# Layer 2's result and layer 3's exponentials turned by way of DRAM, with two small groups and orders of their own for the first and last period

## The chip, the core and the metric

The kernel runs on one core of one Trainium2 chip. A core has five engines with an instruction stream each: the tensor engine (PE), the vector engine (DVE), the scalar engine (ACT), GpSimd (POOL) and the sync engine (SP), which here only issues transfers. Each stream runs in the order in which it was written; between streams there are semaphores. The time is that of the device, in microseconds. Before the change it was 3014.07 (the median of three runs, 3013.18 to 3015.02).

## The reference

Four graph layers run one after the other on 128 independent graphs. A graph has 128 nodes with 256 features (`x`, 128 x 128 x 256, f32) and an adjacency matrix of zeros and ones (`adj`). After every layer stands a residual and a layer norm, `x = norm(x + layer(x))`.

- Layer 0 is graph attention with four heads of 64 features: scores from two vectors per head, leaky relu, a mask by `adj`, softmax, a weighted sum, elu.
- Layer 1 is a gated graph network of three steps. Each step multiplies the state by a weight matrix, sums over neighbours and runs a GRU cell with 256 units. This is most of the arithmetic.
- Layer 2 sums neighbours by relation and multiplies by one matrix per relation, plus a bias. With adjacency values of 0 and 1 only one relation occurs. A general loop behind the main one is run only if a larger value is met.
- Layer 3 is graph attention with one head.

## The kernel before

**Groups and stages.** The 128 graphs go in 32 groups of four (`G`, L25). A group passes four stages, each a Python generator that yields after every small step: `loads` (L124), `head` (layer 0, L348), `body` (layer 1, L437) and `tail` (layers 2 and 3, L573). Before the first period stand, in straight code, the loading of all weights on SP (L137 to L173), the constants on DVE (score columns of `w0` and `w3`, selection matrices, halved biases, L175 to L202) and `fold_weights` (L208), which multiplies layer 1's three matrices into the GRU's input weights: `wc`.

**The order.** The order of work is written out by hand. `STEPS` (L41) is a string of letters, one per step; `LETTERS` (L46) gives each letter a stage and the group relative to the period. `advance` (L688) runs one step. The same string serves all 36 periods, those at the ends too; steps of groups that don't exist fall out. `fold_weights` stands in one piece before period 0. At the end of the main code (L704) every instruction is tied to the one before it on its engine, so that the written order is each engine's order.

**Turning.** PE contracts over the partition dimension, so the kernel needs many 128 x 128 blocks both ways round. It has two ways. PE transposes against an identity matrix (`transpose`, L85), into PSUM, from where ACT or DVE copies or adds. Or the block goes through DRAM: SP writes it out (`to_dram`, L224), four transfers read it back so that 32 x 32 squares lie rearranged (`from_dram`, L234, `squares`, L98), and one DVE instruction transposes all 32 x 32 squares. `turn_rows` (L240) uses the second way for `x1` and `x3`, and the first for the first group's `x1` and the last group's `x3` (`by_pe`). Layer 0's exponentials also go through DRAM, except in the first group (L388, L392, L406).

**The lines that the change touches most.** At the start of `tail` PE turns the last hidden state `h3T` (`hT`), and DVE adds it to `x1` out of PSUM (L577 to L583). Towards its end PE turns layer 3's exponentials `em` and ACT copies them (L664 to L670). In `body`, whose code the change leaves nearly alone, a step's gates are matmuls of 512 columns (four graphs of 128 nodes), L476 to L481; each is two instructions in the trace. `softmax_unscaled` (L312) holds slope, maximum and exponentials. `layernorm` (L261) holds the statistics on DVE, a power on POOL and the scaling on ACT.

**Buffers.** PSUM has four banks for gates and four for all else. `sq`, where squares arrive, is a ring of four; the DRAM buffers `turn` are a ring of four; `x1` and `x3` have two each, `adj` five. The weights that only the folding needs lie in buffers that tail and body use later (`hr`, `xb`, `x3T_0`, `wh3`, `x2_0`).

Of the kernel before, what the change touches and what calls it, by code (L numbers as in the profile page):

```python
# [16 lines left out]
P = 128  # L17
# [22 lines left out]
AHEAD, BEHIND = 2, 2  # L40
STEPS = """  # L41
ucnbbmbggggcbbuucugcglggcccccbbbblbbbbgbbtbuubbbggbbbbggutbttbbubbbbtuttuububutubbbbbbbbgbttggttubbu
uubguhttttbubgtguubbbbbuubtttbbbtbttbttthggggghhhhhhgbhhbbhtgbbbbbbbbgbbbbbbbggghthghtbgggbbbgbtbbtt
ttttbtttbbbbbbbbbbbbbbhghbgthhub
"""
LETTERS = {"b": ("b", 0), "c": ("b", -1), "h": ("h", 2), "g": ("h", 1), "l": ("l", 2), "m": ("l", 1), "n": ("l", -1), "t": ("t", -1), "u": ("t", -2)}  # L46
ORDER = [LETTERS[s] for s in STEPS if s in LETTERS]

@with_exitstack
def kernel(ctx: ExitStack, tc: tile.TileContext, a: dict, out: bass.AP):
# [3 lines left out]
    NG = B // G  # L56
# [50 lines left out]
    def load_adj(st):  # L107
        st["adj"] = ring(sp, [P, G, N], I32, "adj", f"adj_{st['g']}", 5)
        nc.sync.dma_start(st["adj"], adj[st["graphs"]].rearrange("g n m -> n g m"))

    def load_rows(st):
        st["x0"] = sp.tile([P, G, D], F32, tag="x0", name=f"x0_{st['g']}")
        nc.sync.dma_start(st["x0"], x[st["graphs"]].rearrange("g n d -> n g d"))

    def load_x_squares(st):
        st["x0s"] = sp.tile([P, C, G * N], F32, tag="x0s", name=f"x0s_{st['g']}")
        for c in range(C):
            squares(st["x0s"][:, c, :], x[st["graphs"]].rearrange("g n d -> (g n) d")[:, ts(c, P)])

    def load_adj_squares(st):  # L120
        st["adj_s"] = sp.tile([P, G * N], I32, tag="adj_s", name=f"adj_s_{st['g']}")
        squares(st["adj_s"], adj[st["graphs"]].rearrange("g n m -> (g n) m"))
# [7 lines left out]
    def state(g):  # L130
        return {"g": g, "graphs": slice(g * G, (g + 1) * G), "relations": 1, "first": g == 0, "last": g == NG - 1}
# [3 lines left out]


    w0 = cp.tile([P, C, D + 2 * H], F32, tag="w0", name="w0")  # L137
    nc.sync.dma_start(w0[:, :, :D], a["L0_gnn_W"].rearrange("(c p) o -> p c o", p=P))
    vec = ring(sp, [P, 4, D], F32, "y", "vec", 2)
    nc.sync.dma_start(vec[:, 0, :], a["L0_gnn_a_src"].rearrange("h f -> (h f)").partition_broadcast(P))  # L140
    nc.sync.dma_start(vec[:, 1, :], a["L0_gnn_a_dst"].rearrange("h f -> (h f)").partition_broadcast(P))
    load_x_squares(states[0])
    load_adj(states[0])

    w1 = []
    for l, tag in enumerate(("hr", "xb", "x3T_0")):
        w1.append(sp.tile([P, C, D], F32, tag=tag, name=f"w1_{l}"))
        nc.sync.dma_start(w1[l], a["L1_gnn_weight"][l].rearrange("(c p) o -> p c o", p=P))
    wih = []
    for e, tag in enumerate(("wh3", "x2_0")):  # L150
        wih.append(sp.tile([P, 3 * D], F32, tag=tag, name=f"wih_{e}"))
        nc.sync.dma_start(wih[e], a["L1_gnn_w_ih"][e * P : (e + 1) * P, :])
    load_rows(states[0])
    whh = cp.tile([P, C, 3 * D], F32, tag="whh", name="whh")
    nc.sync.dma_start(whh, a["L1_gnn_w_hh"].rearrange("(c p) o -> p c o", p=P))
    bih = cp.tile([P, 3 * C], F32, tag="bih", name="bih")
    nc.sync.dma_start(bih, a["L1_gnn_b_ih"])
    bhh = cp.tile([P, 3 * C], F32, tag="bhh", name="bhh")
    nc.sync.dma_start(bhh, a["L1_gnn_b_hh"])
    w3 = cp.tile([P, C, D + 2], F32, tag="w3", name="w3")  # L160
    nc.sync.dma_start(w3[:, :, :D], a["L3_gnn_W"].rearrange("(c p) o -> p c o", p=P))
    nc.sync.dma_start(vec[:, 2, :], a["L3_gnn_a"][0, :D].partition_broadcast(P))
    nc.sync.dma_start(vec[:, 3, :], a["L3_gnn_a"][0, D:].partition_broadcast(P))
# [3 lines left out]
    def load_w2(t, r):  # L167
        nc.sync.dma_start(t, a["L2_gnn_weight"][r].rearrange("(c p) o -> p c o", p=P))
        return t

    load_w2(w2, 0)
    b2 = cp.tile([P, D], F32, tag="b2", name="b2")
    nc.sync.dma_start(b2, a["L2_gnn_bias"].partition_broadcast(P))  # L173

    for i in range(4):  # L175
        for c in range(C):
            w, nh = (w0, H) if i < 2 else (w3, 1)
            prod = ring(sp, [P, D], F32, "n", f"prod_{c}_{i}", 2)
            nc.vector.tensor_mul(prod, w[:, c, :D], vec[:, i, :])
            lo = D + i % 2 * nh  # L180
            nc.vector.tensor_reduce(w[:, c, lo : lo + nh], prod.rearrange("p (h f) -> p h f", h=nh), AX.X, ALU.add)

    identb = cp.tile([P, P], BF16, tag="identb", name="identb")
    nc.vector.tensor_copy(identb, ident)
    picks = {}
    for S in (G * H, G):
        one = ring(sp, [3 * S, S], F32, "pick", f"one_{S}", 2)  # L190
        nc.vector.tensor_add(one, ident[: 3 * S, :S], ident[: 3 * S, S : 2 * S])
        nc.vector.tensor_add(one, one, ident[: 3 * S, 2 * S : 3 * S])
        picks[S] = cp.tile([3 * S, S, P], BF16, tag=f"pick{S}", name=f"pick_{S}")
        nc.vector.tensor_copy(picks[S], one.unsqueeze(2).to_broadcast([3 * S, S, P]))


    bhalf = cp.tile([P, 2 * C], F32, tag="bhalf", name="bhalf")
    nc.vector.tensor_add(bhalf, bih[:, : 2 * C], bhh[:, : 2 * C])
    nc.vector.tensor_scalar(bhalf, bhalf, 0.5, None, ALU.mult)

    bhn = cp.tile([P, C], F32, tag="bhn", name="bhn")
    nc.vector.tensor_scalar(bhn, bhh[:, 2 * C :], 0.5, None, ALU.mult)  # L202

    wc = cp.tile([P, L, C, 3 * D], F32, tag="wc", name="wc")

    def fold_weights():  # L208
        for l in range(L):
            w1T = ring(sp, [P, C, D], F32, "agT", f"w1T_{l}", 4)  # L210
            for e in range(C):
                ps = bank(C, P)
                for c in range(C):
                    transpose(ps[:, c, :], w1[l][:, c, ts(e, P)])
                nc.scalar.copy(w1T[:, e, :].rearrange("p (c d) -> p c d", c=C), ps)
            for c in range(C):
                for lo, hi in ((0, 512), (512, 3 * D)):
                    ps = bank(hi - lo)
                    for e in range(C):
                        matmul(ps, w1T[:, e, ts(c, P)], wih[e][:, lo:hi], start=e == 0, stop=e == C - 1)  # L220
                    nc.vector.tensor_copy(wc[:, l, c, lo:hi], ps)


    def to_dram(name, *parts):  # L224

        d = ring(dp, [sum(part.shape[1] for part in parts) * P, P], F32, "turn", f"d_{name}", 4)
# [13 lines left out]
    def turn_rows(st, x, tag, name, bufs, by_pe):  # L240

        if by_pe:
            yield
            yield
            t = ring(sp, [P, C, G * N], F32, tag, name, bufs)
            for c in range(C):
                ps = bank(G, N)
                for g in range(G):
                    transpose(ps[:, g, :], x[:, g, ts(c, P)])
                nc.scalar.copy(t[:, c, :].rearrange("p (g n) -> p g n", g=G), ps)  # L250
        else:
# [4 lines left out]
            t = ring(sp, [P, C, G * N], F32, tag, name, bufs)  # L256
# [4 lines left out]
    def layernorm(y, st, name, bufs=1):  # L261

        g0 = st["g"]
        sums = ring(sp, [P, G, 6], F32, "st", f"st_{name}_{g0}", 4)
        mv = ring(sp, [P, G, 2], F32, "mv", f"mv_{name}_{g0}", 4)
        rs = ring(sp, [P, G], F32, "rs", f"rs_{name}_{g0}", 4)
        mr = ring(sp, [P, G], F32, "mr", f"mr_{name}_{g0}", 4)

        def half(k):
            for g in range(k, k + 2):  # L270
                nc.vector.bn_stats(sums[:, g, :], y[:, g, :])  # L271

        def rest():
            for g in range(G):
                nc.vector.bn_aggr(mv[:, g, :], sums[:, g, :])
            nc.vector.tensor_scalar(rs, mv[:, :, 1], EPS, None, ALU.add)
            nc.gpsimd.tensor_tensor(rs, rs, neghalf[:, :G], ALU.pow)  # L277
# [3 lines left out]
            o = st[name] = ring(sp, [P, G, D], F32, name, f"{name}_{g0}", bufs)  # L281
            for g in range(G):
                nc.scalar.activation(  # L283
                    o[:, g, :], y[:, g, :], AF.Identity, bias=mr[:, g : g + 1], scale=rs[:, g : g + 1]
                )
# [5 lines left out]
    def residual_elu_norm(y, xin, st, name, layer, bufs=1):  # L291
# [3 lines left out]
        halves = [slice(k, k + 2) for k in range(0, G, 2)]  # L295
        ts_ = []
        for s in halves:
            t = ring(sp, [P, 2, D], F32, "elu", f"elu_{layer}_{g0}_{s.start}", 2)
            ts_.append(t)
            nc.vector.tensor_scalar(t, y[:, s], 0.0, None, ALU.min)  # L300
            yield
            nc.scalar.activation(t, t, AF.Exp)
            yield
        for s, t in zip(halves, ts_):
            nc.vector.scalar_tensor_tensor(t, y[:, s], 0.0, t, ALU.max, ALU.add)  # L305
            nc.vector.scalar_tensor_tensor(y[:, s], t, -1.0, xin[:, s], ALU.add, ALU.add)  # L306
            yield
            half(s.start)
# [3 lines left out]
    def softmax_unscaled(em, nm, den, cols):  # L312
# [4 lines left out]
        for r, i in enumerate(range(cols.start, cols.stop)):  # L317
# [3 lines left out]
            if r % 4 == 3:  # L321
                yield

    def as_rows(st, cols, name):

        h = cols.shape[2]
        t = ring(sp, [P, 3, G, h], BF16, "split", f"split_{name}", 2)
        r = ring(sp, [P, G, h], F32, "rest", f"rest_{name}", 2)
# [7 lines left out]
        nc.tensor.transpose(ps, t.rearrange("p k g h -> p (k g h)"), identb)  # L336
# [5 lines left out]
    def absent(adj_t, name):  # L342
        nbias = ring(sp, [P, G, N], F32, "nbias", f"nbias_{name}", 2)
# [4 lines left out]
    def head(st):  # L348

        g0, adj_t = st["g"], st["adj"]  # L350
        by_pe = st["first"]
        xT = sp.tile([P, C, G * N], F32, tag="x0T", name=f"x0T_{g0}")
# [4 lines left out]
        if st["relations"] < R:  # L357
            above = sp.tile([P, G, N], F32, tag="adj_T", name=f"above_{g0}")
            nc.scalar.activation(above, adj_t, AF.Relu, bias=negone, accum_out=unmet[:, g0 : g0 + 1])
        yield  # L360
        wh = sp.tile([P, G, D + 2 * H], F32, tag="wh0", name=f"wh0_{g0}")
        for g in range(G):
            ps = bank(D + 2 * H)
            for c in range(C):
# [408 lines left out]
```

## Time and profile before

| | us |
|---|---|
| median of three runs | 3014.07 |
| profiled execution | 3011.99 |
| its span, from the first to the last instruction | 3010.1 |
| PE busy | 2935.0 |
| DVE busy | 1974.9 |
| ACT busy | 1335.4 |
| POOL busy | 494.2 |
| transfers on queue 1 | 34.7% of 16 engines |

A row of the profile names the line of the code, the engine, the operation, the tile written and the tiles read, the shapes and how often it occurs; then the busy time, the mean of one in nanoseconds, the idle time of the engine just ahead of it and what ended that. PEld is PE's loading of the stationary operand, beside the matmuls. "L83" and "L86" are the helpers `matmul` and `transpose`, so the tiles tell such rows apart: `ps<-ident,h3T` is the turning of the last hidden state, `gate<-agT,wc` a gate's part from the neighbours. `SPq` is a transfer issued from SP. In a timeline, several equal instructions in a row are one line: start, time from the first start to the last end, engine, line, operation and count. Ends of matmuls are modelled; starts are measured.

### The profile page before, as it was taken

How to read it: one execution, taken by the hardware profiler on the slowest of the kernel's cores; microseconds unless marked ns; L12 is line 12 of the kernel's file. 1: busy time of each engine (PE TensorE's matmuls, PEld its weight loads, DVE VectorE, ACT ScalarE, POOL GpSimd, SP SyncE). 2: the span in 40 equal slices, each digit the busy share in tenths (PEclk: the TensorE clock that was granted, in tenths of full speed). 3: DMA queues.
4: the chain of work that ended last, by engine and by line, in shares of the span. 5: the costliest groups of instructions: out<-in, count | busy, mean ns of one | idle time of the engine just before them, and what ended most of it. 6: DMA issues, size and time to landing. Idle time of an engine off the chain costs nothing.

```text
span 3010.1 us, 33610 instructions
## 1 busy us (share of the span) xinstructions
PE 2935.0 (98%) x11166; PEld 1707.9 (57%) x11166; DVE 1974.9 (66%) x4393; ACT 1335.4 (44%) x3307; POOL 494.2 (16%) x456
## 2 busy tenths in 40 slices
PE   4999999999999999999999999999999999999995
PEld 3555556555556555556555556555556555556553
DVE  4556676766676766676766676766676766666654
ACT  2344444444444444444444444444444444444433
POOL 0011111111111111111111111111111111111111
PEclk7999999999999999999999999999999999999997
DMA  3243433334433333423343423333433343433310
GB/s 86 39 74 67 84 64 67 60 74 74 84 63 67 60 75 73 84 63 67 60 76 72 85 63 67 60 76 71 84 64 67 60 76 72 84 63 67 63 29 15
DMA packets 902614, 203.24 MB, mean 68 GB/s; under 512 B 723617, under 2 KB 901921, under 8 KB 902433
## 3 DMA queue, kind: packets, MB, share of 16 engines
q1 hardware_dynamic: 902432, 201.01, 34.7%
q8 instruction: 90, 1.47, 0.2%
q14 instruction: 92, 0.75, 0.1%
HBM read 119.15 MB, written 81.79 MB: 67 GB/s over the span
## 4 chain that ended last, share of the span: by engine, by line
PE 97%; DVE 1%; ACT 0%; SPq 0%; issue 0%; DMA 0%; POOL 0%; DVEq 0%; ACTq 0%; POOLq 0%
PE gate L83 66%; PE ps L83 27%; PE ps L86 4%; PE psb L336 0%; DMA vec<-in_L_gnn_a_dram 0%; ACT em L318 0%; SPq L102 0%; DVE em L382 0%; DVE st_x L271 0%; DVE elu L305 0%; DVE y L306 0%; DVE em L314 0%; DVE nm L315 0%; POOL rs_x L277 0%; DVE y L677 0%
## 5 line engine op out<-in xcount | busy, mean ns | idle before, releaser
L83 PE MATMUL gate<-agT,wc 128*128 128x512 f32 x2304 | 1098.8, 592 | 0.8 <-DVE agT L434 0.8
L83 PEld LDWEIGHTS gate<-agT,wc 128*128 128x128 f32 x2304 | 427.6, 190 | 438.6 <-issue 415.7
L83 PE MATMUL gate<-h2T,whh 128*128 128x512 f32 x768 | 372.6, 601 | 0.0
L83 PE MATMUL gate<-h1T,whh 128*128 128x512 f32 x768 | 366.3, 592 | 0.0
L83 PE MATMUL gate<-h0T,whh 128*128 128x512 f32 x768 | 361.0, 592 | 0.0
L318 ACT ACTIVATE em<-em,nm 128x128 f32<-128x128 f32 x640 | 247.0, 388 | 211.4 <-DVE nm L315 211.4
L494 DVE SCALAR_TENSOR_TENSOR n<-r,n 128x512 f32<-128x512 f32 x192 | 132.2, 689 | 209.1 <-ACT n L492 209.1
L508 DVE SCALAR_TENSOR_TENSOR d<-z,d 128x512 f32<-128x512 f32 x192 | 132.3, 689 | 186.8 <-ACT z L486 114.4
L283 ACT ACTIVATE x<-y,mr_x,rs_x 128x256 f32<-128x256 f32 x384 | 199.0, 590 | 84.2 <-DVE mr_x L279 83.9
L500 ACT ACTIVATE n<-n,bih 128x512 f32<-128x512 f32 x192 | 138.1, 719 | 209.7 <-DVE n L498 209.0
L502 POOL TENSOR_TENSOR d<-h2T,n 128x512 f32<-128x512 f32 x64 | 81.3, 1270 | 897.5 <-ACT n L500 897.5
L83 PEld LDWEIGHTS gate<-h0T,whh 128*128 128x128 f32 x768 | 140.9, 190 | 152.6 <-issue 152.3
L434 DVE COPY agT<-ps 128x512 f32<-128x512 f32 x192 | 129.9, 676 | 146.5 <-PE ps L83 146.4
L83 PEld LDWEIGHTS gate<-h2T,whh 128*128 128x128 f32 x768 | 138.3, 190 | 144.1 <-issue 138.7
L83 PEld LDWEIGHTS gate<-h1T,whh 128*128 128x128 f32 x768 | 138.5, 190 | 137.7 <-issue 130.3
L486 ACT ACTIVATE z<-gate,bhalf 128x512 f32<-128x512 f32 x192 | 130.7, 681 | 188.0 <-PE gate L83 188.0
L83 PEld LDWEIGHTS ps<-wh,aT 128*128 128x128 f32 x1280 | 174.5, 196 | 41.7 <-issue 22.0
L492 ACT ACTIVATE n<-gate,bhn 128x512 f32<-128x512 f32 x192 | 131.5, 685 | 139.0 <-PE gate L83 139.0
L83 PE MATMUL ps<-wh,aT 128*128 128x64 f32 (+1 forms) x1280 | 187.3, 299 | 5.8 <-DVE aT L404 4.9
L486 ACT ACTIVATE r<-gate,bhalf 128x512 f32<-128x512 f32 x192 | 131.6, 685 | 101.3 <-PE gate L83 101.3
L502 POOL TENSOR_TENSOR d<-h0T,n 128x512 f32<-128x512 f32 x64 | 86.6, 1352 | 529.6 <-ACT n L500 529.6
L498 DVE TENSOR_TENSOR n<-n,gate 128x512 f32<-128x512 f32 x192 | 131.6, 685 | 50.9 <-PE gate L83 47.4
(112 smaller groups left out, 4025.8 us busy)
## 6 DMA issues: line engine op xcount, KB each, us to landing
d_em<-em SPq DMA_DIRECT2D x62, 512.0 KB, 3.4
sq_em<-d_em SPq DMA_DIRECT2D x248, 128.0 KB, 4.3
x0s<-in_x_dram SPq DMA_DIRECT2D x256, 64.0 KB, 2.6
x<-in_x_dram SPq DMA_DIRECT2D x32, 512.0 KB, 4.1
out_dram<-o SPq DMA_DIRECT2D x32, 512.0 KB, 4.4
d_h0T<-x SPq DMA_DIRECT2D x62, 256.0 KB, 2.8
sq_h0T<-d_h0T SPq DMA_DIRECT2D x124, 128.0 KB, 3.5
d_x3T<-x SPq DMA_DIRECT2D x62, 256.0 KB, 2.7
```

The source lines that it names most:

```text
L83: nc.tensor.matmul(ps, lhsT, rhs, start=start, stop=stop)
L86: nc.tensor.transpose(ps, src, ident)
L283: nc.scalar.activation(o[:, g, :], y[:, g, :], AF.Identity, bias=mr[:, g : g + 1], scale=rs[:, g : g + 1])
L318: nc.scalar.activation(em[:, r, :], em[:, r, :], AF.Exp, bias=nm[:, i : i + 1], accum_out=den[:, i : i + 1])
L434: nc.vector.tensor_copy(into[c], ps.rearrange("p g n -> p (g n)"))
L486: nc.scalar.activation(t, gate[name][0], AF.Tanh, bias=bhalf[:, col : col + 1], scale=0.5)
L492: nc.scalar.activation(n, gate["nh"][0], AF.Identity, bias=bhn[:, c : c + 1], scale=0.5)
L494: nc.vector.scalar_tensor_tensor(n, tr, 1.0, n, ALU.add, ALU.mult)
L498: nc.vector.tensor_add(n, n, gate["ni"][0])
L500: nc.scalar.activation(n, n, AF.Tanh, bias=bih[:, 2 * C + c : 2 * C + c + 1])
L502: nc.gpsimd.tensor_sub(d, hT[:, c, :], n)
L508: nc.vector.scalar_tensor_tensor(d, tz, 1.0, d, ALU.add, ALU.mult)
```

## The change

1. **Sizes.** The groups are now one of two graphs, 31 of four, one of two: 33. All tiles and loops take the group's own size `n`; where a step has nothing to do in a small group, it yields all the same.
2. **h3 by way of DRAM.** In all groups but the last, SP writes the two halves of `h3T` to DRAM and reads them back as squares, DVE transposes them, and POOL adds `x1` in two instructions. The last group still turns on PE.
3. **em3 by way of DRAM.** The same for layer 3's exponentials: one write, four reads, one DVE instruction, which takes the place of four PE transposes and ACT's copy. The last group still uses PE.
4. **Orders.** The first period (`START`) and the last (`END`) have strings of their own, and the middle (`STEPS`) a new one in which more stages overlap: tails of the groups 1, 2 and 3 back, heads of this group and the two ahead.
5. **Constants and folding as stages.** They are generators too, letters in `START`, so that their steps stand between those of the first heads.
6. **Queues.** The first group's loads come first on SP; all weights are issued from ACT.
7. **Small things.** `turn` becomes a ring of eight; `x3T` and `h0T` have one buffer each; the split of the scores is filled with zeros first in a small group.

```diff
-AHEAD, BEHIND = 2, 2
+FIRST = {"a": ("c", 0), "b": ("f", 0), "c": ("l", 0), "d": ("h", 0), "e": ("l", 1), "f": ("h", 1), "g": ("l", 2), "h": ("b", 0), "i": ("h", 2)}
+START = """
+abcbaaccabadbdaadddddddddaabeeacddadabbbbbbbbbbddbddbbdbbbbbbfbbbbbbbbdddddddddddgddddbbddddddfbbfdd
+dddddffffdbfffffffdfddddfdgfhdfffehfbhhhfffffhhhhhhhhhhhhhfhhfhhhhhhfihhhhhhhfhhhhhhhhffhhhhhiffhhhh
+hhhhhhfhhfhfhhhhhhhffffhihhhhhiffbiffhihffhbfiihfiihihhihhhh
+"""
+PERIOD = {"a": ("t", -2), "b": ("h", 0), "c": ("l", 2), "d": ("b", -1), "e": ("h", 1), "f": ("b", 0), "g": ("t", -3), "h": ("h", 2), "i": ("t", -1), "j": ("l", 1), "k": ("l", 0)}
 STEPS = """
...
+LAST = {"a": ("t", -3), "b": ("b", -2), "c": ("h", -1), "d": ("t", -4), "e": ("b", -1), "f": ("t", -2), "g": ("t", -1), "h": ("l", -1)}
+END = """
...
@@
-    NG = B // G
+    sizes = [2] + [G] * ((B - 4) // G) + [2]
+    NG = len(sizes)
+    spans = [slice(sum(sizes[:i]), sum(sizes[: i + 1])) for i in range(NG)]
@@
+        by_pe = {"head": g == 0, "tail": g == NG - 1}
+        return {"g": g, "graphs": spans[g], "n": sizes[g], "relations": 1, "by_pe": by_pe}
@@
+    load_x_squares(states[0])
+    load_adj(states[0])
+    load_rows(states[0])
+
     w0 = cp.tile([P, C, D + 2 * H], F32, tag="w0", name="w0")
-    nc.sync.dma_start(w0[:, :, :D], a["L0_gnn_W"].rearrange("(c p) o -> p c o", p=P))
+    nc.scalar.dma_start(w0[:, :, :D], a["L0_gnn_W"].rearrange("(c p) o -> p c o", p=P))
...
+    def constants(st):
+        def score_columns(w, nh, i):
+            for c in range(C):
...
+                yield
+        yield from score_columns(w0, H, 0)
+        yield from score_columns(w0, H, 1)
...
+        yield from score_columns(w3, 1, 2)
+        yield from score_columns(w3, 1, 3)
+    def fold(st):
         for l in range(L):
...
                 for c in range(C):
                     transpose(ps[:, c, :], w1[l][:, c, ts(e, P)])
+                yield
                 nc.scalar.copy(w1T[:, e, :].rearrange("p (c d) -> p c d", c=C), ps)
+                yield
...
                         matmul(ps, w1T[:, e, ts(c, P)], wih[e][:, lo:hi], start=e == 0, stop=e == C - 1)
+                    yield
                     nc.vector.tensor_copy(wc[:, l, c, lo:hi], ps)
+                    yield
@@
-        d = ring(dp, [sum(part.shape[1] for part in parts) * P, P], F32, "turn", f"d_{name}", 4)
+        d = ring(dp, [sum(part.shape[1] for part in parts) * P, P], F32, "turn", f"d_{name}", 8)
@@ def tail(st):
-        for c in range(C):
-            ps = bank(G, N)
-            for g in range(G):
-                transpose(ps[:, g, :], hT[:, c, ts(g, N)])
-            yield
-            nc.vector.tensor_add(y[:, :, ts(c, P)], ps, x1[:, :, ts(c, P)])
...
+        else:
+            d = ring(dp, [n * C * P, P], F32, "turn", f"d_h3_{g0}", 8)
+            for c in range(C):
+                nc.sync.dma_start(
+                    d.rearrange("(g c p) m -> c p g m", c=C, p=P)[c], hT[:, c, :].rearrange("p (g m) -> p g m", g=n)
+                )
+            yield
+            s = from_dram(f"h3_{g0}", d)
+            yield
+            y = ring(sp, [P, n, D], F32, "y", f"y1_{g0}", 2)
+            nc.vector.transpose(y.rearrange("p g d -> p (g d)"), s)
+            yield
+            for k in range(0, n, 2):
+                nc.gpsimd.tensor_add(y[:, k : k + 2], y[:, k : k + 2], x1[:, k : k + 2])
             yield
...
-        aT = sp.tile([P, G, N], F32, tag="aT3", name=f"aT3_{g0}")
-        ps = bank(G, N)
-        for g in range(G):
-            transpose(ps[:, g, :], em[:, g, :])
-        yield
-        nc.scalar.copy(aT, ps)
-        yield
+        aT = sp.tile([P, n, N], F32, tag="aT3", name=f"aT3_{g0}")
+        if by_pe:
...
+        else:
+            d = to_dram(f"em3_{g0}", em)
+            yield
+            s = from_dram(f"em3_{g0}", d)
+            yield
+            nc.vector.transpose(aT.rearrange("p g n -> p (g n)"), s)
+            yield
@@
-    for p in range(-AHEAD, NG + BEHIND):
-        if p == 0:
-            fold_weights()
-        for which, ahead in ORDER:
+    for which, g in order(START, FIRST):
+        advance(which, g)
+    for p in range(1, NG - 1):
+        for which, ahead in order(STEPS, PERIOD):
             advance(which, p + ahead)
+    for which, g in order(END, LAST):
+        advance(which, NG + g)
```

In `START`, `a` are the constants, `b` the folding, `d`, `f` and `i` the heads of groups 0, 1 and 2, `h` the body of group 0, and `c`, `e`, `g` their loads. In `END`, `a`, `f` and `g` are the tails of groups 30, 31 and 32, `b` and `e` the bodies of groups 31 and 32, `c` the head of group 32.

## The prediction

> **What bounds the kernel now.** I read the page's first two parts, then the same busy times by stretch, then the tensor engine's groups with shapes kept apart, then its timeline and those of the other engines.
>
> ```profile
> span 3010.1 us, 33610 instructions
> PE 2935.0 (98%) x11166; PEld 1707.9 (57%) x11166; DVE 1974.9 (66%) x4393; ACT 1335.4 (44%) x3307; POOL 494.2 (16%) x456
> ```
>
> ```profile
> 0.00:28.00 28.00, 0.00 (x0) 0.00 (x0) 10.06 (x29) 2.10 (x3) 0.79 (x8) 1.00 0.63 183
> 28.00:71.00 43.00, 28.27 (x112) 21.69 (x113) 23.25 (x59) 14.35 (x52) 1.03 (x1) 0.69 0.14 31
> 71.00:91.30 20.30, 19.78 (x65) 11.49 (x64) 7.38 (x15) 2.60 (x7) 0.00 (x0) 0.90 0.00 0
> 91.30:2952.00 2860.70, 2859.91 (x10896) 1656.42 (x10895) 1906.24 (x4214) 1296.71 (x3198) 483.28 (x438) 1.00 0.36 68
> 2952.00:3010.00 58.00, 27.08 (x98) 18.25 (x96) 28.00 (x79) 19.66 (x49) 9.11 (x9) 0.74 0.06 20
> ```
>
> Columns: stretch, its length, busy PE, PEld, DVE, ACT, POOL, clock, DMA share, GB/s. From 91.3 to 2952 PE is free for 0.8 us in all; before and after, it waits. So a matmul removed from the middle counts in full, and the ends are chains of other engines.
>
> Ends of matmuls are modelled, so I cost PE work by distances between starts.
>
> ```profile
> 1262.26 0.60 PE L86 MATMUL ps<-ident,h3T 128*128 128x128 f32 x4
> 1262.70 1.88 PE L83 MATMUL gate<-agT,wc 128*128 128x512 f32 x4
> 1264.41 1.88 PE L83 MATMUL gate<-h0T,whh 128*128 128x512 f32 x4
> 1270.00 0.60 PE L86 MATMUL ps<-ident,em 128*128 128x128 f32 x4
> 1270.44 0.60 PE L86 MATMUL ps<-ident,h3T 128*128 128x128 f32 x4
> ```
>
> Four transposes take 0.44 us (110 ns each; the row's 273 ns is latency), four 512-column gates 1.72 (429 ns). So counted, a group's matmuls sum to 89.6 us; a period measures 90.25 (the first edge matmuls start at 1155.31 and 1245.56), 0.65 being small waits.
>
> **PE work.** Each inner group loses 8 h3 transposes (L580) and 4 of em3 (L667): 12 x 0.110 = 1.32 us; 31 groups: **-40.9**. At the ends the old first group turns em (16) and x1 (8) on PE, the old last group x3, em3 and h3 (20): 44. The groups of two need 12 and 10. 22 x 0.11 = -2.4; the small fixed parts done by two half groups instead of one full one, +0.3. Sum **-43.0**. A half group's gates have 256 columns: 0.216 us each by the w,hr matmuls (eight in 1.73), so half.
>
> **What replaces it,** per period of 90 us: DVE loses two adds (1.37) and gains transposes of 1.24 and 0.66, +0.5, on 61 busy; ACT loses a copy of 0.6; POOL gains two adds of 1.27 on 15. SP gains 11 issues: 2 writes (0.93) and 4 reads (2.3) for h3, 1 and 4 (2.7) for em3, 6 us on some 26. Nothing of this is PE, so its price is nothing while the data arrive in time. Moved are all steps, in new orders; in the middle I laid the written PE steps on a clock by these distances. SP there meets, in order: squares of x, h0T's write and reads, out, em0's write, h3's write, em3's write, h3's reads, em3's reads. h3's reads stand behind em3's write, which waits for layer 3's exponentials, at about 27.6; they are issued from 28.1 to 30.4 and land by 34 (h0T's reads: 3.5 us). DVE wants them at 39.5. So **5.5 us of slack** hide the h3 leg. em3's reads land at 36 for 44.4; behind them on SP stand em0's reads, wanted 30 us later.
>
> Here stands a rule against the change: the Trainium skill, "DMA: Bandwidth & Descriptors", section "Rules for kernel authors", sends transposes by DMA to the hardware form, not a rearranged access pattern, with a factor of 19. Taken as the speed of h3's 512 KB reads at a nineteenth of that page's 436 GB/s, an estimate, they need 23 us and every period loses 17: 500 us slower. But this trace has the same pattern:
>
> ```profile
> sq_h0T<-d_h0T SPq DMA_DIRECT2D x124, 128.0 KB, 3.5
> sq_x3T<-d_x3T SPq DMA_DIRECT2D x124, 128.0 KB, 3.6
> DMA packets 902614, 203.24 MB, mean 68 GB/s; under 512 B 723617, under 2 KB 901921, under 8 KB 902433
> ```
>
> Queue 1 keeps 16 engines 34.7% of 3010 us busy with 902,432 packets: 18.5 ns each. The new legs have 7,680 a period (h3: 1,024 rows of 512 B written, 4,096 runs of 128 B read; em3 half of each): 8.9 us of sixteen engines, a share of 37% becoming 47%. I take the row.
>
> **Where slack is thin.** Two places on that clock. (1) em3's DVE transpose stands behind the POOL adds of y1 and the update of h1T c1, ends at 45.3 and PE wants it at 45.4. (2) h2T c0 stands behind the adds of y2 and their statistics: 3.8 us on DVE plus two hand-offs of 0.25, against 4.3 us of PE work. At (1) a second rule bears, the skill's "SBUF — State Buffer", section "SBUF: two separate sides": DVE instructions with two SBUF inputs and GpSimd reads exclude each other for a whole instruction. The row:
>
> ```profile
> 1280.36 1.10 DVE L509 SCALAR_TENSOR_TENSOR h1T<-d,n 128x512 f32<-128x512 f32 x1
> 1280.16 3.25 POOL L592 TENSOR_TENSOR xb<-x,b 128x256 f32<-128x256 f32 x4 [3.39 <-ACT x L283]
> ```
>
> 0.41 more than its 0.69 under a POOL add of 0.85. By the rule a 1.27 us add costs up to 1.27 a period, 38 us in 30; by the row's half of the competing add 0.6, or 18; the two overlap by only about 0.35 on my clock. I take 0.25 per period, **+7.5** (ends: 0, since old waits of 0.65 are kept, and 30).
>
> **The start.** Lost is here time less PE work done, at full clock. Old: the DVE stands 12.9 us before the last score vector, behind which the first transpose waits.
>
> ```profile
> 20.88 0.42 DVE L179 TENSOR_TENSOR prod<-w,vec 128x256 f32<-128x256 f32 x1 [12.91 <-DMA vec<-in_L_gnn_a_dram]
> 26.73 1.24 DVE L353 STREAM_TRANSPOSE x0T<-x0s 128x1024 f32<-128x1024 f32 x1
> 28.03 6.84 PE L83 MATMUL ps<-w,x0T 128*128 128x264 f32 x16 [28.03 <-DVE x0T L353]
> 71.40 1.11 PE L86 MATMUL ps<-ident,w 128*128 128x128 f32 x4
> 91.29 1.95 PE L83 MATMUL ps<-edge,x 128*128 128x128 f32 x16
> ```
>
> Head until 71, then the fold alone until 91.3. By then 32.0 us of PE work are done (head 10.9, the next head 4.3, fold 16.8): 59.3 lost. New: x's squares are first on SP, weights on ACT. ACT computes nothing before its 17th issue: at best at 9 us (17 of SP's 0.45, 0.9 more for whh), at worst 17.9 as on SP. 4.2 MB at the first slices' 236 GB/s are 18 us and the last was issued some 4 before it landed: 14. Then its table load (1.3), copies and the mask reach 17.6; DVE splits the scores at 19.1, after two products of the late vectors. Fold pieces fill PE; the 264-column matmuls above took 428 ns against 221 later, so cold work costs double, and the first pick's sums start at 25.5. Half a head then: sums 2.2, a fold copy 0.7, slope and maximum 2.4, exponentials 3.2, transposes and copies 2.5, weighted sums 1.9, scaling 0.9, elu to norm 6.6: body 0 starts at **46**. The written first order has 36.2 us of PE work left, and 6.2 of waits: exponentials of group 1 ahead of body 0's first tanh on ACT, and em0's reads on SP behind its second write, landing near 69 while DVE stands. It ends at 88.4 with 62.9 of work done: 25.5 lost. **-33.8** (ends: -26 with a cold clock throughout, -42 with ACT free at 9).
>
> **The end.** Old: after the last gate (2952.98) 57.1 us with 15.3 of work, 41.9 lost. New: the last order has 71.1 us of PE work. Body 32's first matmul comes at 17.3; to its last gate are 45 of work and some 11 of waits (1.2 for agT behind the last h3T, 0.8 for agT10, 1.0 for the norm before rel, 1.6 around w2, 2.2 for agT11 behind y2, 4.1 for h2T behind tail 31's norms and elu): 73.2. Its own tail, old stages halved where they scale: update to rel 7.7 (old 8.8), to y2 6.2 (8.8), to x3's turn 3.4 (3.9), to wh 2.5 (2.6), to split 3.1 (5.6), to em3 2.0 (1.8), to the exponentials' end 2.8 (4.1), turn 3.0 (1.4; tail 31's output norm stands ahead on ACT), sum 1.7 (2.1), elu to norm 6.1 (9.6), norm 1.2 (2.1), store 6.4 (6.4): 46. Total 119, 47.9 lost: **+6.0** (ends -6, +15). The cover of body 32 is only two tails.
>
> **Sum.** 3010.1 - 43.0 - 33.8 + 6.0 + 7.5 = 2946.8 us of span. The profiled execution took 3011.99, 1.9 over its span; the median shown, 3014.07, is 2.1 over that. **2951 us**, 2.1% less.
>
> **Rivals.** (a) Both ends shorter: start 8 better, end 10 better, thin places free (7.5): 2925. For it: the middle now loses under 0.65 a period in just such orders. (b) Thin places cost 0.8 more a period: 2951 + 24 = 2975. For it: DVE's 1.48 us maximum on a 0.69 elu step beside POOL. (c) The transposes ran in time PE could not use; the period stays 90.25: 2951 + 41 = 2992. Against: 0.44 us between starts with no gap. (d) Slower: one mechanism, h3's reads late on SP because em3's write ahead of them waits for exponentials. Beyond the slack PE loses what they are late. To undo 63 us in 30 periods takes 2.1 us each, so they decide once they land 7.6 us later than I have them; at 8.0, 0.4 x 30 more, 3026. Against: SP issues for 32 us of 90.
>
> **How the numbers follow.** Likeliest 55%, own range 2937 to 2965; (a) 18%, (b) 18%, (c) 4%, (d) 5%. From 2920 to 2980 a third of (a) and of (b) and all of (c) and (d) stay outside, 2 in 10. 0.2% (6 us) is what a measurement of this kernel tells from no change: faster 95% (all but (d)), within 1%, slower 4%, the last two dividing (d).
>
> **What would show it.** Period from start to start of one step: 88.9 to 89.2 (90.25 in (c), 90 in (b)). No matmul with h3T and ident but four at the end. Body 0's first matmul near 46, body 1 under way by 90. PE waits, if any, on T of em3 and on h2T. From the last gate to the end 46. It is wrong if PE is idle in the middle for more than 0.5 us a period, or if ACT starts after 18.

## The result and the profile after

The changed kernel takes **2967.93 us** (median of four runs, 2965.38 to 2971.45) against 3013.99 for the kernel before in the same session: a ratio of 0.9848, 95% interval 0.9831 to 0.9865. It is 46 us faster where 63 were forecast: inside the range of 2920 to 2980, 3 us outside the likeliest case's own (2937 to 2965). The profiled execution is the slowest of the four, 2971.45, with a span of 2969.7.

The page of the changed kernel, busy times:

```profile
span 2969.7 us, 34231 instructions
PE 2898.6 (98%) x10918; PEld 1691.9 (57%) x10918; DVE 2026.4 (68%) x4456; ACT 1326.1 (45%) x3310; POOL 564.7 (19%) x529
```

PE has fewer matmuls, 10918 in place of 11166. The same kernel by stretches: the start up to body 0's first matmul, the rest of the first order, the middle, the last order up to the last gate, its own tail (columns as before):

```profile
0.00:28.00 28.00, 11.91 (x24) 6.68 (x25) 11.62 (x36) 3.24 (x8) 0.79 (x8) 1.00 0.82 192
28.00:50.80 22.80, 20.89 (x104) 14.43 (x102) 17.17 (x41) 7.98 (x30) 0.72 (x1) 1.00 0.28 59
50.80:94.00 43.20, 39.76 (x209) 33.65 (x206) 29.06 (x68) 20.24 (x67) 4.53 (x5) 0.96 0.33 61
94.00:2856.00 2762.00, 2743.90 (x10250) 1576.86 (x10249) 1906.77 (x4145) 1251.17 (x3103) 538.50 (x492) 1.00 0.43 87
2856.00:2931.70 75.70, 68.20 (x291) 50.84 (x290) 42.53 (x106) 31.14 (x77) 14.88 (x16) 0.95 0.22 44
2931.70:2969.70 38.00, 13.91 (x52) 9.46 (x50) 19.27 (x61) 12.31 (x29) 5.25 (x7) 0.68 0.18 50
```

The middle had 0.8 us of idle PE before; it now has 18 (2762.0 less 2743.9, by modelled ends). The waits of PE in the changed kernel, total, times and longest, say where:

```profile
PE ps L101 <- DVE aT L751: 13.5, 28, 0.5
PE ps L104 <- DMA w<-in_L_gnn_weight_dram: 9.5, 1, 9.5
PE ps L101 <- DVE aT L454: 4.0, 2, 2.9
PE ps L104 <- DVE h2T L558: 3.9, 2, 3.7
PE ps L101 <- DVE rel L672: 3.6, 1, 3.6
PE ps L101 <- DVE x0T L391: 3.6, 1, 3.6
```

The first row comes once in nearly every period: the matmuls with layer 3's weights wait for em3's DVE transpose (L751). The others are single events at the ends or in the periods next to them. From start to start of one step a period is **89.70 us** (edge matmuls at 1074.81 and 1164.51), against 90.25 before. The period's chain at that place, from the timelines of DVE, POOL, ACT and PE:

```profile
1104.97 1.21 DVE L648 STREAM_TRANSPOSE y<-sq_h 128x1024 f32<-128x1024 f32 x1
1107.72 1.64 DVE L557 SCALAR_TENSOR_TENSOR d<-z,d 128x512 f32<-128x512 f32 x1 [1.55 <-ACT z L535]
1109.39 0.69 DVE L558 SCALAR_TENSOR_TENSOR h1T<-d,n 128x512 f32<-128x512 f32 x1
1110.00 0.70 DVE L751 STREAM_TRANSPOSE aT<-sq_em 128x512 f32<-128x512 f32 x1
...
1106.32 2.49 POOL L651 TENSOR_TENSOR y<-y,x 128x512 f32<-128x512 f32 x2 [0.77 <-DVE y L648]
...
1106.93 0.69 ACT L535 ACTIVATE z<-gate,bhalf 128x512 f32<-128x512 f32 x1 [1.19 <-PE gate L101]
...
1109.25 1.02 PE L101 MATMUL gate<-agT,wc 128*128 128x512 f32 x2
1110.76 1.13 PE L101 MATMUL ps<-wh,aT 128*128 128x256 f32 x4 [0.49 <-DVE aT L751]
```

DVE turns h3 (L648); POOL then runs the two adds y1+x1 until 1108.81. Meanwhile z is ready at 1107.62 and DVE starts the update's first instruction (L557), which takes 1.64 us in place of 0.69. em3's transpose stands behind the update. The two gate matmuls before the wait need 0.86 us, so PE was ready for the next ones at 1110.11 and starts them at 1110.76: 0.66 lost (1.086 from start to start in place of 0.429), and 0.10 more shows on the matmul after. That is 0.76 a period. The reads themselves are in good time: the last one of h3 is issued by 1095.75 and has landed at 1099.13, and DVE wants it at 1104.97; em3's have landed by 1100.53, 9.5 us before their transpose starts.

### The profile page after: what moved, and what is told of

The parts are those of the page before. It is cut to its first block, busy times and chain, and to the rows that moved or that the text cites. A ratio compares the mean times of both kernels' runs of the same rounds, so it can differ in the third digit from the quotient of the medians.

```text
span 2969.7 us, 34231 instructions
## 1 busy us (share of the span) xinstructions
PE 2898.6 (98%) x10918; PEld 1691.9 (57%) x10918; DVE 2026.4 (68%) x4456; ACT 1326.1 (45%) x3310; POOL 564.7 (19%) x529
## 3 DMA queue, kind: packets, MB, share of 16 engines
q1 hardware_dynamic: 1157536, 248.87, 41.9%
## 4 chain that ended last, share of the span: by engine, by line
PE 92%; DVE 4%; issue 1%; ACT 1%; DMA 1%; POOL 0%; DVEq 0%; SPq 0%; ACTq 0%; POOLq 0%
PE gate L101 63%; PE ps L101 27%; PE ps L104 2%; DVE d L557 2%; DVE aT L751 1%; ACT z L535 1%; PE psb L375 0%; DMA wih<-in_L_gnn_w_ih_dram 0%; DMA x<-in_x_dram 0%; ACT em L353 0%; DVE em L349 0%; DMA d_h0T<-x 0%; ACT x L316 0%; DVE st_x L303 0%; DMA vec<-in_L_gnn_a_src_dram 0%
## 5 line engine op out<-in xcount | busy, mean ns | idle before, releaser
L101 PE MATMUL gate<-agT,wc 128*128 128x512 f32 (+1 forms) x2376 | 1116.3, 583 | 3.3 <-DVE agT L483 3.3
L101 PE MATMUL gate<-h2T,whh 128*128 128x512 f32 (+1 forms) x792 | 375.9, 584 | 0.0
L101 PE MATMUL gate<-h1T,whh 128*128 128x512 f32 (+1 forms) x792 | 373.7, 581 | 0.0
L101 PE MATMUL gate<-h0T,whh 128*128 128x512 f32 (+1 forms) x792 | 362.5, 580 | 1.3 <-DVE h0T L289 1.3
L557 DVE SCALAR_TENSOR_TENSOR d<-z,d 128x512 f32<-128x512 f32 (+1 forms) x198 | 159.8, 807 | 270.9 <-ACT z L535 227.3
L543 DVE SCALAR_TENSOR_TENSOR n<-r,n 128x512 f32<-128x512 f32 (+1 forms) x198 | 132.9, 671 | 265.4 <-ACT n L541 265.3
L535 ACT ACTIVATE z<-gate,bhalf 128x512 f32<-128x512 f32 (+1 forms) x198 | 132.7, 670 | 257.0 <-PE gate L101 256.9
L551 POOL TENSOR_TENSOR d<-h2T,n 128x512 f32<-128x512 f32 (+1 forms) x66 | 82.8, 1255 | 751.7 <-ACT n L549 751.7
L309 POOL TENSOR_TENSOR rs_x<-rs_x,neghalf 128x4 f32<-128x4 f32 (+1 forms) x99 | 108.4, 1095 | 612.3 <-DVE rs_x L308 612.2
L549 ACT ACTIVATE n<-n,bih 128x512 f32<-128x512 f32 (+1 forms) x198 | 139.6, 705 | 174.4 <-DVE n L547 172.9
L535 ACT ACTIVATE r<-gate,bhalf 128x512 f32<-128x512 f32 (+1 forms) x198 | 132.3, 668 | 190.2 <-PE gate L101 190.1
L101 PE MATMUL ps<-wh,aT 128*128 128x64 f32 (+1 forms) x1280 | 191.8, 297 | 17.9 <-DVE aT L751 13.5
L483 DVE COPY agT<-ps 128x512 f32<-128x512 f32 (+1 forms) x198 | 129.0, 652 | 113.2 <-PE ps L101 113.2
L541 ACT ACTIVATE n<-gate,bhn 128x512 f32<-128x512 f32 (+1 forms) x198 | 133.2, 673 | 146.7 <-PE gate L101 146.7
L551 POOL TENSOR_TENSOR d<-h0T,n 128x512 f32<-128x512 f32 (+1 forms) x66 | 82.1, 1244 | 528.0 <-ACT n L549 528.0
```

The source lines that it names most:

```text
L101: nc.tensor.matmul(ps, lhsT, rhs, start=start, stop=stop)
L309: nc.gpsimd.tensor_tensor(rs, rs, neghalf[:, :n], ALU.pow)
L483: nc.vector.tensor_copy(into[c], ps.rearrange("p g n -> p (g n)"))
L535: nc.scalar.activation(t, gate[name][0], AF.Tanh, bias=bhalf[:, col : col + 1], scale=0.5)
L541: nc.scalar.activation(n, gate["nh"][0], AF.Identity, bias=bhn[:, c : c + 1], scale=0.5)
L543: nc.vector.scalar_tensor_tensor(n, tr, 1.0, n, ALU.add, ALU.mult)
```

## The experiments

My theory after this reading: POOL's adds keep DVE's two-input update out, em3's transpose is late by it, and this one place eats most of what the turns by DRAM save. The rivals: em3's transfers are late; DVE's queue is merely too long there; or the saving itself is less than its 1.32 us. For the start: ACT issues loads too long.

All times below are medians of four or five runs; ratios are to the kernel before on the same chip, with 95% intervals. "Period" is the distance from the start of one step to its start a period later.

| kernel | us | ratio | period |
|---|---|---|---|
| changed kernel again | 2967.25 | 0.9846 (0.9833 to 0.9860) | 89.70 |
| em3's transpose first | 2946.06 | 0.9781 (0.9768 to 0.9795) | 88.94 |
| y1+x1 on DVE | 2946.79 | 0.9785 (0.9771 to 0.9798) | 88.94 |
| h3 on PE | 2974.17 | 0.9872 (0.9857 to 0.9887) | 89.81 |
| em3 on PE | 2959.43 | 0.9820 (0.9806 to 0.9833) | 89.38 |
| both on PE | 2988.12 | 0.9915 (0.9901 to 0.9928) | 90.25 |
| transpose first, again | 2946.12 | 0.9776 (0.9763 to 0.9789) | 88.94 |
| and late weights on SP | 2942.33 | 0.9768 (0.9755 to 0.9781) | 88.94 |
| the same, again | 2944.55 | 0.9770 (0.9757 to 0.9783) | 88.94 |
| and two steps at the ends | 2942.19 | 0.9767 (0.9754 to 0.9780) | 88.94 |
| a third POOL add | 2991.93 | 0.9929 (0.9912 to 0.9945) | 90.58 |

**The base.** No edit.

> The changed kernel once more, as the measure for the runs beside it: some 2968 us, 0.985 of the kernel before. Its middle repeats every 89.70 us, and once in each period TensorE waits for em3's DVE transpose, 0.66 us with 0.10 more on the matmul behind it.

2967.25, as expected.

**em3's transpose first.** One letter of `STEPS` moves one place past the update:

```diff
-aiiiefafffffaaffieiiafaifiiififaiaaaijfiifafaafafffiffiieffiiiikefffiaiifefaefffafiafefafffeefffehff
+aiiiefaffffafaffieiiafaifiiififaiaaaijfiifafaafafffiffiieffiiiikefffiaiifefaefffafiafefafffeefffehff
```

> em3's DVE transpose goes ahead of h1T c1's update on DVE. Theory (the update is held up by POOL's y1+x1 adds, and the transpose stands behind it): DVE has 1.55 us free there, so the 0.66 + 0.10 us of TensorE go away in 29 periods, 22 us; the period falls from 89.70 to 88.94, the time to 2946. First rival (em3's reads are what is late): nothing or some us worse. Second rival (the next thin place, h1T c1 or h2T c0 on TensorE, takes over the wait): between 0 and 22 us.

2946.06 and a period of 88.94: both numbers of the theory. DVE and POOL in this kernel:

```profile
1096.75 0.67 DVE L751 STREAM_TRANSPOSE aT<-sq_em 128x512 f32<-128x512 f32 x1
1098.37 1.64 DVE L557 SCALAR_TENSOR_TENSOR d<-z,d 128x512 f32<-128x512 f32 x1 [0.95 <-ACT z L535]
1100.05 0.69 DVE L558 SCALAR_TENSOR_TENSOR h1T<-d,n 128x512 f32<-128x512 f32 x1
...
1096.97 2.50 POOL L651 TENSOR_TENSOR y<-y,x 128x512 f32<-128x512 f32 x2 [0.76 <-DVE y L648]
```

The update is as slow as before, 1.64; only nothing urgent stands behind it. Between 270 and 2650 us PE waits for nothing in this kernel, so the next thin place did not take it over. The transfers were not late either: the transpose now runs 31.3 us after the period's first edge matmul, where it ran at 35.2, and waits for nothing. For 0.45 us it ran beside POOL's first add, and neither took longer (0.67, and 2.50 for the two adds), so it is not kept out.

**y1+x1 on DVE.**

```diff
-                nc.gpsimd.tensor_add(y[:, k : k + 2], y[:, k : k + 2], x1[:, k : k + 2])
+                nc.vector.tensor_add(y[:, k : k + 2], y[:, k : k + 2], x1[:, k : k + 2])
```

> The order stays and h3's residual adds (y1+x1) run on DVE in place of POOL. Theory (exclusion between POOL's adds and the update's two-input DVE instruction): DVE's own 1.4 us of adds end as z comes, so the update takes 0.69 again in place of 1.64, the transpose is 0.9 us earlier, and the 22 us go as in the run with the transpose first: 2946. Rival (the DVE queue is simply too long there): 1.4 us more work ahead of the transpose, so the wait stays or grows by up to 0.5 us a period: 2968 to 2985.

2946.79. DVE in this kernel:

```profile
1095.96 1.29 DVE L651 TENSOR_TENSOR y<-y,x 128x512 f32<-128x512 f32 x2
1097.48 0.69 DVE L557 SCALAR_TENSOR_TENSOR d<-z,d 128x512 f32<-128x512 f32 x1 [0.22 <-ACT z L535]
1098.20 0.69 DVE L558 SCALAR_TENSOR_TENSOR h1T<-d,n 128x512 f32<-128x512 f32 x1
1098.81 0.70 DVE L751 STREAM_TRANSPOSE aT<-sq_em 128x512 f32<-128x512 f32 x1
```

DVE has 1.3 us more to do ahead of the update and is done sooner: the update is back at 0.69. A queue that is merely too long would have made it worse. So the cause is shown from two sides: leave the collision and move what waits behind it, or leave the order and take the collision away.

**A third POOL add.** To price the exclusion, one more add behind the two, into the buffer of `xb`, which is free there; nothing reads it.

```diff
+            idle = sp.tile([P, n, D], F32, tag="xb", name=f"idle_{g0}")
+            nc.gpsimd.tensor_add(idle[:, :2], y[:, :2], x1[:, :2])
```

> The changed kernel with one POOL add more behind y1+x1 in every inner group, of the same two operands and size (1.27 us), into a tile that nothing reads. Theory (a POOL add that runs keeps DVE's two-input update out until the adds end): the update starts its work 1.27 us later, em3's transpose and TensorE with it: period 89.70 to 90.97, 29 times, 3005. Rival (the update gets in between two adds, or only shares the memory with them): the update waits no longer than now, period 89.70, 2968.

2991.93, between the two: the period grows by 0.88, not by 1.27 and not by nothing. DVE and POOL in this kernel show why:

```profile
1112.26 1.56 DVE L557 SCALAR_TENSOR_TENSOR d<-z,d 128x512 f32<-128x512 f32 x1 [1.55 <-ACT z L535]
1113.86 1.64 DVE L558 SCALAR_TENSOR_TENSOR h1T<-d,n 128x512 f32<-128x512 f32 x1
...
1110.79 2.48 POOL L651 TENSOR_TENSOR y<-y,x 128x512 f32<-128x512 f32 x2 [0.70 <-DVE y L648]
1113.23 1.71 POOL L653 TENSOR_TENSOR idle<-y,x 128x512 f32<-128x512 f32 x1
```

The update's first instruction waits out the second add only, and then goes; the third add now takes 1.71 in place of 1.27, since it waits for DVE; the update's second instruction waits for the third add, 1.64 in place of 0.69. So the two engines take turns, one instruction each. My theory had the update held until all adds end, which was wrong; the rival, that it slips in between, holds for one instruction and not for the pair.

**h3 on PE again.** In `tail` every group takes the way of the last one:

```diff
-        if by_pe:
+        if True:
             yield
             yield
             y = ring(sp, [P, n, D], F32, "y", f"y1_{g0}", 2)
```

> h3 alone is turned on TensorE again in every group: 8 transposes, 0.88 us a period, come back, and its adds read PSUM on DVE, so that POOL's adds go. Theory: the 0.76 us that TensorE loses at em3's transpose go with POOL's adds, so the period gains only 0.12: 29 to 31 periods, 4 us slower than the changed kernel, 2972. Rival (the lost time has nothing to do with h3's turn): 0.88 x 31 = 27 us slower, 2995.

2974.17, 7 us above the changed kernel, near the theory's 4 and far from 2995. Turning h3 by DRAM removed 0.88 us of PE work a period and brought 0.76 of waiting. The period grows by 0.11, some 3 us of the 7; where the rest lies was not traced.

**em3 on PE again.** The same condition at `aT3`, and the letter of the turn five places earlier, ahead of z's last matmuls:

```diff
         aT = sp.tile([P, n, N], F32, tag="aT3", name=f"aT3_{g0}")
-        if by_pe:
+        if True:
...
-aiiiefafffffaaffieiiafaifiiififaiaaaijfiifafaafafffiffiieffiiiikefffiaiifefaefffafiafefafffeefffehff
+aiiiefaafffffaffieiiafaifiiififaiaaaijfiifafaafafffiffiieffiiiikefffiaiifefaefffafiafefafffeefffehff
```

> Layer 3's exponentials alone are turned on TensorE again in every group, 5 us of TensorE work ahead of the sums that want them; h3 stays on the way through DRAM and POOL adds y1+x1 as in the changed kernel. Theory: the four transposes cost 0.44 us a period and the 0.76 that TensorE lost at em3's DVE transpose go, since nothing behind the update is wanted so soon: period 89.70 to 89.38, time 2958. Rival (the wait only moves, to the update's own reader): 0.44 x 31 = 14 us slower than the changed kernel, 2981.

2959.43: faster than the changed kernel with 0.44 us more of PE work in each period.

**Both on PE again.** The edits of the last two runs together.

> Both turns, h3's and em3's, are back on TensorE in every group; groups of 2 at the ends, both end orders and the constants as stages stay. Theory: 0.88 + 0.44 - 0.76 = 0.56 us a period more than the changed kernel's 89.70, 90.26, which is the period of the kernel before; 30 of them make 2985. What is left against the kernel before, 28 us, is the worth of the ends. Rival (the turns through DRAM gave the whole gain and the ends nothing): 3013.

2988.12 and the old period, 90.25. So of the 46 us, 25 are the ends' (3013.53 less 2988.12) and 21 the two turns'. Which part of the 25 comes from the small groups, the orders, the stages or the queues, no run separates. With the transpose first, the turns are worth 42 (2988.12 less 2946.12), near the 40.9 forecast.

**The start.** The base with the transpose first, and then late weights from SP:

> The kernel with em3's DVE transpose ahead of the update once more, as the measure for the next run: 2946, the period 88.94.

```diff
-        nc.scalar.dma_start(w1[l], a["L1_gnn_weight"][l].rearrange("(c p) o -> p c o", p=P))
+        queue = nc.scalar if l == 0 else nc.sync
+        queue.dma_start(w1[l], a["L1_gnn_weight"][l].rearrange("(c p) o -> p c o", p=P))
...
-    nc.scalar.dma_start(whh, a["L1_gnn_w_hh"].rearrange("(c p) o -> p c o", p=P))
+    nc.sync.dma_start(whh, a["L1_gnn_w_hh"].rearrange("(c p) o -> p c o", p=P))
...
-    load_w2(w2, 0, nc.scalar)
+    load_w2(w2, 0)
...
-    nc.scalar.dma_start(b2, a["L2_gnn_bias"].partition_broadcast(P))
+    nc.sync.dma_start(b2, a["L2_gnn_bias"].partition_broadcast(P))
```

> Over the run with the transpose first, ACT issues eleven loads instead of sixteen, with the small ones and layer 3's weights ahead; w1 of relations 1 and 2, whh, w2 and b2 go to SP behind group 0's own loads. Theory (the start is late because ACT, which computes nothing until its last issue at 18.8 us, is late with the copies of w1T and wh): ACT's first computing instruction at 11 to 13 in place of 19.35, the first split's transpose at 20 in place of 24.8, body 0's first matmul at 46.5 in place of 50.9, and the time 4 us less, 2942. Rival (DVE's wait for the squares of x and the mask, or TensorE's half speed up to 30 us, sets the start): ACT is earlier, the split at most 1 us, the time the same within 2 us.

ACT and PE in the changed kernel, ACT with its issues (ACTq):

```profile
8.44 1.54 ACTq L169 DMA_DIRECT2D w<-in_L_gnn_weight_dram  x2
13.31 0.60 ACTq L181 DMA_DIRECT2D w<-in_L_gnn_W_dram  x1
18.84 0.48 ACTq L193 DMA_DIRECT2D b<-in_L_gnn_bias_dram  x1
19.35 1.28 ACT L244 ACT_TABLE_LOAD   x1 [19.35 <-DMA vec<-in_L_gnn_a_dram]
...
14.14 3.89 PE L101 MATMUL ps<-w,x0T 128*128 128x264 f32 x8 [3.58 <-DVE x0T L391]
21.07 3.78 PE L101 MATMUL ps<-wih,w1T 128*128 128x512 f32 x4 [3.04 <-ACT w1T L244]
24.78 0.30 PE L375 MATMUL psb<-identb,split 128*48 128x128 bf16 x1
...
50.89 1.26 PE L101 MATMUL ps<-edge,x 128*128 128x128 f32 x4
```

ACT and PE with the late weights on SP:

```profile
12.67 0.44 ACTq L184 DMA_DIRECT2D vec<-in_L_gnn_a_dram  x1
13.14 1.28 ACT L245 ACT_TABLE_LOAD   x1 [13.14 <-DMA bhh<-in_L_gnn_b_hh_dram]
...
13.70 3.88 PE L101 MATMUL ps<-w,x0T 128*128 128x264 f32 x8 [2.77 <-DVE x0T L392]
17.38 2.86 PE L101 MATMUL ps<-wih,w1T 128*128 128x512 f32 x4
21.45 0.24 PE L376 MATMUL psb<-identb,split 128*48 128x128 bf16 x1 [1.21 <-DVE split L372]
...
46.47 1.26 PE L101 MATMUL ps<-edge,x 128*128 128x128 f32 x4
```

Between these two traces ACT computes 6 us sooner, PE goes from the heads' matmuls into the folding with no gap, the split's transpose comes 3.3 us sooner and body 0's first matmul 4.4. But the start differs from one execution to the next, and the first of these two is the latest of its kind. Over all traces, with sixteen loads on ACT that matmul stands at 47.9 to 50.9 us in nine executions (median 48.4), with eleven at 44.8, 45.4 (the kernel of the next run) and 46.5 in three. So some 3 us are shown there. The time, 2942.33 and 2944.55 in two sets against 2946.06 and 2946.12, agrees with 3, but its intervals overlap, and 4 were expected.

**Two steps at the ends.** The last kernel again as the base, and then one line each of `START` and `END`:

> The kernel with the transpose first and the late weights on SP once more, as the measure for the next run: 2942, body 0's first matmul at 46.5 us.

```diff
-abcbaaccabadbdaadddddddddaabeeacddadabbbbbbbbbbddbddbbdbbbbbbfbbbbbbbbdddddddddddgddddbbddddddfbbfdd
+abcbaaccabadbdaadddddddddabeecdaadadabbbbbbbbbbddbddbbdbbbbbbfbbbbbbbbdddddddddddgddddbbddddddfbbfdd
...
-fffaaeaeefffafeaaaaafffffeeeffafefeefeeeeaaeffeeeeeeeeaeeeeeeeeeeeeeeeeeefefafeeefffeffeffeefeeeefgg
+fffaaeaeefffafeaaaaafffffeeeffafefeeeeeeeeefaaffeeeeeeaeeeeeeeeeeeeeeeeeefefafeeefffeffeffeefeeeefgg
```

> Two more steps of the written orders at the ends. At the start DVE splits group 0's scores ahead of layer 3's score vectors, whose loads it had waited 2.42 us for; at the end ACT takes body 32's tanh of n and z ahead of the second half of tail 31's norm, and DVE the update of h2T c0 ahead of tail 30's elu. Theory: the split's transpose no longer waits for DVE, only for the folds ahead of it, 21.45 to 20.2; TensorE's wait for h2T falls from 3.66 to 2.3; together 2.6 us, 2939.7. Rival (both ends have a second chain as long): under 1 us, 2942.

2942.19. The split's transpose, at 20.35, no longer waits; but the base has it at 21.45 in one execution and at 19.75 in the other, so its time alone says nothing. The wait for h2T falls from 3.67 to 2.52, a little less than expected. From body 32's first matmul to its last gate the last order took 55.7 and 58.0 us in the two executions of the base, with granted clocks of 1.00 and 0.94 in that stretch, and 55.5 here with 1.00. At equal clock, then, nearly all of the shorter wait comes back elsewhere in the stretch, which is what the rival said. The intervals of the times are those of the base, so the expected 2.6 us are not shown. The kernel beats both kernels of the comparison, as does every one with the transpose first.

## Why the prediction was right, and where it was off

By its own steps, in spans: start to 88.4, then the middle, then 119 for the end; measured 93.6, 2762.4 and 113.7.

- **PE work, -43.0: right.** The period would have been 88.93 (90.25 less 1.32), and with the wait gone it is 88.94. Four h3 transposes remain, at the end, as forecast.
- **The h3 leg's slack, 5.5 us: right.** At the place shown it was 5.8 (landing 1099.13, reader 1104.97), and 5.5 or more in 30 of the 32 groups that turn h3 so (the other two, near the ends, had 3.9 and 1.7). Queue 1 has 1,157,536 packets, 255,104 more than before, and a DMA share of 0.43 in the middle for the 0.47 expected. The row of the same pattern was the right measure and the factor of 19 was not: the reads of h3 land 3.2 us after their issue, median of 128. Rival (d) did not come near.
- **Thin place (1), 0.25 a period: the right place, the wrong size.** It is 0.76 in nearly every one of 29 periods, 20.8 us by distances between starts, for the 7.5 written down. Two sizes were off. On my clock POOL's adds and the update overlapped by 0.35; they overlap by 1.1. And I took half of the competing add by one row of the trace, where the rule of the Trainium skill, "SBUF — State Buffer", section "SBUF: two separate sides", is that the pair goes to whichever instruction starts first, for the whole of it. The measured 0.95 of stretch is about the rest of the add that was running, 1.09 by the records. The rule's 1.27 a period, 38 us, is more than was lost: the add had run for some 0.2 us when the update came, and 0.2 of the 0.95 fell into slack (0.76 lost). That is rival (b), 0.51 over my term in place of its 0.8. The period, 89.70, lies outside the 88.9 to 89.2 forecast and near (b)'s 90.
- **Thin place (2), h2T c0: nothing there.** No wait of PE on it in the middle.
- **The middle in all: +23.** About 13 of it is that wait (20.8 for 7.5). With em3's transpose first, a trace with the same dip of the clock takes 2741.1 for this stretch, 21.3 less. The other 10 are not the wait's: PE waits 2.9 at 2756.8 for the transpose of layer 0's exponentials (L454), 1.3 and 0.5 before 107 us, and half clock for 6.8 us behind the first of these costs 3.4. My sum has no term for these places. Some 1.6 us stay open.
- **The start, -33.8: about 5 too good** (in this execution; with the same first order others end it 2 to 6 us later than forecast). ACT was put at 14 and computes at 19.35; I had given 17.9 as the worst. There are sixteen issues, not seventeen, and most take under half a microsecond, as counted. What was missing are the pauses between them, up to 3.5 us (13.91 to 17.38); that the queue takes no more issues then is my reading, and the trace doesn't show what ACT waits for. The text named ACT after 18 as a sign of being wrong, and it was one. Body 1's first matmul is at 98.8 rather than "by 90".
- **The end, +6.0: 5 too bad.** Body 32's first matmul came at 17.24 of the last order (17.3 forecast), its last gate at some 75.5 (73.2), and its own tail took 38 us in place of 46: the turn of em3 1.0 for 3.0, the store 4.4 for 6.4, the update to rel 6.3 for 7.7, rel to y2 5.0 for 6.2, and small ones.

So start and end nearly cancelled, by luck, and what separates 2951 from 2968 is thin place (1) with the periods next to the ends. The forecast's other sign of being wrong, more than 0.5 us of idle PE a period, came up too: 0.66.

That h3's turn is worth 7 us alone and em3's is worth less than nothing in this kernel (2959.43 without it) was not among the rivals. Each was costed by the matmuls it removes, while the wait needs both: h3's turn puts the adds on POOL, and em3's puts a reader behind the update.

## What to carry to other kernels

Work moved to an idle engine is not free where it can keep out an engine that has a deadline, as POOL's adds did DVE's update: look which instruction it can hold up and what is queued behind it, and if the queue's order is free, put the urgent step first. Here one letter in the order was worth as much as the change's 21 us of turns by DRAM. Where two edits meet at one wait, undo each alone and both together before crediting either.

## What the runs showed of the hardware

**What is kept out and what is not.** In the changed kernel's trace, DVE instructions of 512 columns or more that overlapped a POOL add or difference of two SBUF tiles (L551, L651, L661), against the same ones beside none:

| DVE instruction | alone, median ns | beside POOL: count, mean extra, longest |
|---|---|---|
| update, two SBUF inputs (L557) | 692 | 29, +911, 1642 |
| leaky relu of em3, two SBUF inputs (L349) | 688 (two only) | 29, +1004, 1699 |
| minimum for elu, one SBUF input (L332) | 418 | 60, +272, 957 |
| copy from PSUM (L483) | 677 | 60, -23, 693 |
| PSUM and SBUF inputs (L698) | 682 | 30, +10, 692 |
| transpose of 1024 columns (L454) | 1245 | 29, -11, 1235 |

POOL's power of 128x4 (L309) is another case. The update's second instruction for h2T ran beside it 31 times and took 691 to 693. The first had started some 0.2 us ahead of the power, which then takes 1.33 us in place of 1.01: here it is POOL that waits. So the length of a POOL instruction alone doesn't tell what it keeps out. Between update and adds the turns go instruction by instruction, as the third add showed.

**The clock column is blind ahead of its first record.** The heads' first matmuls of 264 columns start 444 ns apart in the changed kernel (222 in the middle), and after the gap of 3.04 us four folding matmuls start 0.9 us apart instead of 0.43; the column says 1.00 for both. But the trace's records of the granted clock begin only at 27.14 us here, with full clock, and the column counts the time ahead of them as full. In all thirteen traces PE runs at half speed up to the first record and at full speed from it on. Later the records alternate between full and half clock, and the column shows it:

```profile
2730.00:2780.00 50.00, 47.13 (x184) 29.70 (x183) 30.10 (x73) 20.62 (x41) 8.49 (x9) 0.93 0.30 55
```

In this stretch the records give half clock from 2757.80 to 2764.62, behind the wait of 2.9 us at 2756.8. All twelve traces with the new orders have half clock there, for 3.4 us (three) or 6.8 (nine); that makes 1.7 us between executions of one kernel. The Trainium skill, "TensorE: Matmul & The Clock Gate", "Part 1: The HAM clock gate", gives half speed until some 3.4 us of unbroken work and after an idle window as long, with windows that run free of the kernel; the ratio and the lengths agree, though the wait here is shorter than 3.4.

Whether ACT's delay cost PE twice, by the gap and by the speed behind it, shows only in part. From the heads' first matmul to the first record it is 3.1 to 5.8 us in the three traces with no gap behind the heads' matmuls, 3.3 to 9.3 in five with a gap of 0.9 to 1.3, and 8.8 to 13.0 in four with 1.7 to 3.0. In one of the three without a gap the first four folding matmuls take 0.43 each; in the other two the first of them still run at half speed.

**Picks and splits.** The "small waits" of 0.65 a period that I kept are not waits: distances between starts show 0.09 to 0.10 us more at each place where bf16 matmuls (picks, splits) meet f32 ones or a group of them ends, ten of them in the period of the kernel before that starts at 1155.31. These matmuls also have other shapes (48 or 12 rows); no run tells the type from the shape.
